# A graph-and-experts layer on one core: the first two expert lots gathered on chip instead of through DRAM, and the products for nodes without edges spread over two PSUM banks

## The chip, the cores and the metric

One core of one Trainium2 chip runs the kernel. The time is device microseconds of that core, from the start to the end of one execution; six executions of the kernel before are given. A trace of one further execution, taken by the hardware profiler, goes with them. In it PE is TensorE's matmul stream and PEld its weight loads, DVE is VectorE, ACT is ScalarE, POOL is GpSimd, SP is SyncE; a suffix q (ACTq, SPq) is the sequencer of that engine, which issues transfers.

## The reference, cut to what matters

```python
# x: 3125 x 256; src, dst: 100000 edges, sorted by dst
xn = layernorm(x)
e   = relu((xn[dst] - xn[src]) @ theta.T + theta_b + xn[src] @ phi.T + phi_b)
gnn = segment_max(e, dst)                     # one row of 256 per node, 0 where there is no edge
q, k, v = split(xn @ w_qkv.T)                 # 8 heads of 64; k and v are normalised per head
mix = (q @ (k.T @ v) / N) @ w_out.T + b_out   # attention without softmax
x = x + gnn + mix
t = layernorm(x)
p, i = top_k(softmax(t @ Wr + br), 2)         # 2 of 8 experts for each node
y_e  = gelu((t * ln_g[e] + ln_b[e]) @ W1[e] + b1[e]) @ W2[e] + b2[e]   # 256 -> 1024 -> 256
out = x + sum over the two chosen experts of (p / sum p) * y_e
```

## The kernel before

**Tiles and groups.** The 3125 nodes are 25 tiles of 128 rows (`NT`, `P`). They are cut into five groups, worked on from the last nodes to the first: `GROUPS` is ((17,25), (10,17), (4,10), (1,4), (0,1)), called group 0 to group 4 here. The edges are laid out in columns of 128, one edge per partition; group 0 takes 134 columns, the others 151, 185, 158 and 99 (`STEPS`), 727 in all.

**The edge stream.** For each column, POOL gathers 128 rows of a table `b_d` in DRAM by an indirect DMA (`gather`, L129, called at L1663), and DVE folds the row into a running maximum (`fold`, L414), six columns behind (`LAG`). Windows of 8 columns are stored to DRAM (`s_d`) by SP. Five window buffers turn. When the columns of a group are folded, `group(g)` (L1424) sends the group's tiles through `token_tile` (L483: last edge row by an indirect DMA `r1`, maximum, relu, layer norm, router logits), then `dispatch` (L1397) ranks each node among those that chose the same expert (`slots`, L589) and, for groups 0 and 1, scatters the normalised rows by POOL into a table `xs_d` in DRAM, ordered by expert (`scatter`, L136; two halves of a group, one indirect DMA per tile and choice).

**Nodes without edges.** `without_edges` (L454) computes for each tile of 128 nodes, before its tokens are handled, `xn @ theta.T + biases` and `x + mix`: one bias product, two products of 512 columns with `am_w`, and a product of x itself with an identity, which adds x inside PSUM. ACT copies both halves out (L463, L464). The PSUM tile comes from the class `Early` (L1385), which hands out the one bank that the expert stream later uses under the name `trf`.

```python
am = ps.tile([P, 2 * D], F32, name="mm")
add_bias(am, E, P, slice(0, 2 * D), True, False)
for c in range(2):
    nc.tensor.matmul(am, xnT(i, c), am_w[:, c, :], start=False, stop=False)
nc.tensor.matmul(am[:, D:2 * D], ident, x_sb[:, i, :], start=False, stop=True)
```

**The expert stream.** `Stream.go` (L895) works through lots (group, expert), 8 lots for each of groups 0 to 3. A lot has 256 places (128 in group 3). Lots are numbered u in the order they are added: 0 to 7 are group 0, 8 to 15 group 1, 16 to 23 group 2, 24 to 31 group 3. For groups 0 and 1 a pair of lots is loaded from `xs_d` in one DMA of 512 KB issued by ACT (`rows`, L807) and turned by PE transposes (`turn`, L848). For groups 2 and 3 nothing goes through DRAM (`on_chip`, L796): DVE builds a one-hot matrix per tile from the ranks (`hots`, L826), and PE multiplies the normalised rows of the group's tiles with it (`turn`, L837). Both end in the bank `trf`; ACT scales it to `xe` (`scaled`, L859). `Units.run` (L722) then does the expert: for each of 8 chunks f a first product into `hp` (L730), Gelu by ACT (L732), and, interleaved, the second products of the lot before into `yp` (L754). A program-order helper `done` stores the result to `ys_d`. `between` says what else of the next lots is issued at which f. Group 4 (one tile) goes through all 8 experts densely at the end (`dense_tile`, L973), and `combine` (L1564) gathers the stored expert rows back for the other groups.

**What sets the order.** All engines but POOL run in an order written out by hand: tasks are Python generators, each `yield n` means n ticks later, and the loop of the gathers advances the clock `now` by one tick per POOL transfer (`tick`, L1354). So a task's instructions stand on each engine's queue at a place relative to the gathers, and each engine goes through its queue in that order. The expert stream paces itself by a model of PE: `on_pe` (L92) adds an assumed cost in microseconds to `clock["pe"]` (one tick is taken as 1.25 us), and `room` (L763) keeps the stream about two ticks ahead of it. Masks for the highest-degree nodes (`first_maxima`, L1206; PE L1256, DVE L1222) are worked off between, starting when group 0 has been dispatched, and pausing while the tokens of groups 1 and 2 are handled.

**Names that matter below.** `add(g)` (L778) appends a group's 8 lots to the stream; for group 0 it is called at L1476, five ticks after the last scatter. `ring` (L161) holds 14 buffers for Gelu outputs. PSUM holds three tiles `mm`, and for the stream one `trf`, two `hp` and two `yp`.

Of the kernel before, what the change touches and what calls it, by code (L numbers as in the profile page):

```python
# [8 lines left out]
F32 = mybir.dt.float32  # L9
# [5 lines left out]
OP = mybir.AluOpType  # L15
# [4 lines left out]
P = 128  # L20
# [4 lines left out]
D = 256  # L25
# [22 lines left out]
G = len(GROUPS)  # L48
# [19 lines left out]
TICK = 1.25  # L68
ROWS = 256
SPILL = 128  # L70
APART_3 = 32
ROWS_3 = 2 * APART_3 + E + 2

# [7 lines left out]
def gps_layer(ctx: ExitStack, tc: tile.TileContext, x, src, dst, thetaT, phiT, biases, wq, wkvT,  # L81
# [372 lines left out]
    def without_edges(ps, i):  # L454

        am = ps.tile([P, 2 * D], F32, name="mm")
        add_bias(am, E, P, slice(0, 2 * D), True, False)
        for c in range(2):
            nc.tensor.matmul(am, xnT(i, c), am_w[:, c, :], start=False, stop=False)
        nc.tensor.matmul(am[:, D:2 * D], ident, x_sb[:, i, :], start=False, stop=True)  # L460
        on_pe(2.3)
        yield 3
        nc.scalar.copy(xn2(i), am[:, 0:D])  # L463
        nc.scalar.copy(x_sb[:, i, :], am[:, D:2 * D])  # L464

    def roots(work, v, y):

# [121 lines left out]
    def slots(ro, ps, g, half, i0, i1, pick, taken, chosen=None):  # L589
# [36 lines left out]
        over = ro.tile([P, nt, E], F32, name="over")  # L626
        nc.vector.tensor_scalar(over, rank, float(cap), None, op0=OP.is_ge)
        if chosen is not None:
            nc.vector.scalar_tensor_tensor(chosen[:, i0 - first:i1 - first, :], rank, 1.0, took, op0=OP.add, op1=OP.mult)
            clock["chosen", g, half] = True  # L630
            yield 1
# [26 lines left out]
        slot_f = ro.tile([P, 2, nt], F32, name="slot_f")  # L658
        nc.vector.tensor_reduce(slot_f, mine, AX.X, OP.add)
        nc.vector.tensor_scalar(from_i[:, :, i0:i1], slot_f, float(end), None, op0=OP.min)  # L660
        if chosen is not None:
            return
        out2 = ro.tile([P, nt], F32, name="out2")
        nc.vector.tensor_scalar(out2, slot_f[:, 1, :], float(end), float(of_group), op0=OP.is_ge, op1=OP.mult)
# [44 lines left out]
    class Units:  # L709
# [12 lines left out]
        def run(self, e, w1t, xe, w2t, done, between, parts, part):  # L722


            n = parts * part
            hT = []
            for f in range(FC):
                hp = self.ps.tile([P, ROWS], F32, name="hp")
                for c in range(2):
                    nc.tensor.matmul(hp[:, 0:n], w1t[:, c, f, :], xe[:, c, 0:n], start=(c == 0), stop=(c == 1))  # L730
                hT.append(self.hidden())
                nc.scalar.activation(hT[f][:, 0:n], hp[:, 0:n], AF.Gelu, bias=sm[:, 4 + f, e:e + 1])  # L732
                on_pe(n / P * 0.43)
# [33 lines left out]
    class Stream:  # L767


        def __init__(self, wts, act, ps):  # L770
            self.wts, self.act, self.ps = wts, act, ps
            self.lots, self.through, self.open = [], set(), True
            self.held = {}
            self.chosen = {}
            self.parts = []
            self.plan()

# [16 lines left out]
            return xn_hi[:, 7 + 4 * to:11 + 4 * to, :]  # L794

        def on_chip(self, u):  # L796
            return u < len(self.lots) and self.lots[u][0] >= G - 3

        def spilled(self, u):

# [4 lines left out]
                asked.append((G - 3, move(nc.scalar, to, xs_d[at:at + SPILL].rearrange("(p s) d -> p s d", s=2))))  # L805

        def rows(self, v):  # L807
            if 2 * v < len(self.lots) and ("xs", v) not in self.held and not self.on_chip(2 * v):
                xs = self.held["xs", v] = self.at(v % 2)
                asked.append((self.lots[2 * v][0], move(nc.scalar, xs.rearrange("p (k s) d -> p k s d", k=2), self.two(v))))  # L810
                for g, put in sent:
                    if g > asked[-1][0]:
                        apart_in_rows(asked[-1][1], put)

        def hots(self, u):

            if self.on_chip(u) and ("hot", u) not in self.held:
                g, e = self.lots[u]
                n, nt = CAPS[g], GROUPS[g][1] - GROUPS[g][0]
                if g == G - 3:  # L820
                    flat = xn_hi[:, 7:13, :].rearrange("p s d -> p (s d)")
                else:
                    flat = xn_lo[:, 6:9, :].rearrange("p s d -> p (s d)")[:, u % 2 * nt * n:(u % 2 + 1) * nt * n]
                hot = self.held["hot", u] = flat.rearrange("p (i n) -> p i n", n=n)
                for i in range(nt):
                    nc.vector.tensor_scalar(hot[:, i, :], place_of[g], self.chosen[g][:, i, e:e + 1], None, op0=OP.is_equal)  # L826

        def turn(self, u):
            if ("hot", u) in self.held and ("tr", u) not in self.held:
                tr = self.held["tr", u] = self.ps.tile([P, 2, ROWS], F32, name="trf", bufs=1)  # L830
                g = self.lots[u][0]
                i0, i1 = GROUPS[g]
                hot = self.held["hot", u]
                more = self.held.get(("over", u))
                for c in range(2):
                    for i in range(i0, i1):
                        nc.tensor.matmul(tr[:, c, 0:CAPS[g]], xn2(i)[:, c * P:(c + 1) * P], hot[:, i - i0, :],  # L837
                                         start=(i == i0), stop=(i == i1 - 1 and more is None), skip_group_check=True)
                    for r in range(0 if more is None else 2):
                        nc.tensor.matmul(tr[:, c, r * P:r * P + SPILL // 2], more[:, r, c * P:(c + 1) * P],  # L840
                                         ident[0:SPILL // 2, 0:SPILL // 2], start=False, stop=(r == 1), skip_group_check=True)
                on_pe(1.5 if more is None else 6.1)
            elif ("xs", u // 2) in self.held and ("tr", u) not in self.held:
                tr = self.held["tr", u] = self.ps.tile([P, 2, ROWS], F32, name="trf", bufs=1)
                n = self.half(u)
                for c in range(2):
                    for r in range(2):
                        nc.tensor.transpose(tr[:, c, r * n:(r + 1) * n],  # L848
                                            self.held["xs", u // 2][0:n, self.lots[u][1] % 2 * 2 + r, c * P:(c + 1) * P],
                                            ident[0:n, 0:n])  # L850
                on_pe(1.2)
# [43 lines left out]
        def go(self):  # L895
# [5 lines left out]
            while True:  # L901
                if u == len(self.lots):

                    for _ in units.last():
                        yield room()
                    units.behind = None
                    if u < len(self.lots):
                        continue
                    if not self.open:
                        break  # L910
                    if G - 3 in self.through:
                        nc.scalar.activation(table, eps, AF.Sqrt)
                    while u == len(self.lots):
                        yield 0.5
                    nc.scalar.activation(table, eps, AF.Gelu)
                if ("xe", u) not in self.held:
                    self.rows(u // 2)
                    self.spilled(u)
                    self.hots(u)
                    yield 8 if ("hot", u) not in self.held else 4 if ("over", u) in self.held else 1.5  # L920
                    self.turn(u)
                    yield 2
                    self.scaled(u)
                    yield 2
# [460 lines left out]
    class Early:  # L1385

        def tile(self, shape, dt, name):
            return at_hand["ffp"].tile([P, 2, ROWS], dt, name="trf", bufs=1).rearrange("p c n -> p (c n)")

    carried = {}  # L1390
    routed = set()
# [5 lines left out]
    def dispatch(g, half, i0, i1, top, top_i, taken):  # L1397
# [10 lines left out]
        if g >= G - 3:  # L1408
            yield from slots(ro, mm, g, half, i0, i1, made[0], taken, at_hand["ffn"].chosen[g])
            return  # L1410
        yield from slots(ro, mm, g, half, i0, i1, made[0], taken)
        yield BEHIND_SLOTS[g]
        put = []
        for i in range(i0, i1):
# [9 lines left out]
    def group(g):  # L1424
# [11 lines left out]
        if g >= G - 3 and g < G - 1:  # L1436
# [23 lines left out]
        for i in range(i0, i1):  # L1460
            start(routed_tile(i, last_rows(at_hand["tok"], i, rows), slices, carried, top[:, i - i0, :],
                              top_i[:, i - i0, :], newton=g == 1, at_once=2 if g > 1 else None))
            yield PER_TILE[g]
        if g == G - 2:
            while ("chosen", g, 0) not in clock:
                yield 0.5
            at_hand["ffn"].add(g)
            at_hand["ffn"].open = False
# [171 lines left out]
    def mixers():  # L1640
# [195 lines left out]
```

## Time and profile before

| what | value |
|---|---|
| median of 6 runs | 1159.2 us (1158.15 to 1163.15) |
| the profiled execution | 1161.85 us, its span 1160.0 us, granted PE clock 0.899 |
| PE busy | 897.9 us, 77% of the span |
| DVE busy | 793.9 us, 68% |
| POOL busy | 846.1 us, 73% |
| ACT busy | 331.7 us, 29% |
| the chain that ended last | PE 32%, DVE 20%, DMA 19%, POOL 16%, issue 12%, ACT 1% |

The chain's share is spread over four engines, so the span has to be read by stages: mixers and edges up to about 262 us, nodes without edges from 262 to 405 us, then the lots of group 0 (first Gelu at 436.5 us), group 1 (597.7 us), group 2 (814.7 us) and group 3 (1004.2 us), and the dense tile from 1090 us. Those stage starts are the first ACT L732 of each lot in the timeline.

### The profile page before, as it was taken

To read this page: it belongs to the slowest core of one execution; us is meant where nothing else is said; L and a number is where in the kernel's file an instruction comes from. 1 tells how busy PE (TensorE), PEld (TensorE's weight loads), DVE (VectorE), ACT (ScalarE), POOL (GpSimd) and SP (SyncE) were. 2 spreads that over 40 slices of the span, in tenths; PEclk is the share of its full clock that TensorE was granted. 3 is DMA by queue.
4 is the path that set the end of the run, shared out by engine and by line. 5 is a ranking of instruction groups with operands and counts; after the bars stand their busy time and mean duration, and the time that the engine had idled before them with its cause. 6 is when DMAs were issued, how large, how long until landed. Compare 5 with 4: busy or idle time off the path is not lost.

```text
span 1160.0 us, 14777 instructions
## 1 busy us (share of the span) xinstructions
PE 897.9 (77%) x4461; PEld 691.4 (60%) x4461; DVE 793.9 (68%) x2543; ACT 331.7 (29%) x799; POOL 846.1 (73%) x868
## 2 busy tenths in 40 slices
PE   6436888846567609989958898844999998999896
PEld 5323444423244208867747787733877786898796
DVE  7599998874567327587358787776888866733542
ACT  4310233311133103243222232331312224333342
POOL 6677777777777777777777777777777777776461
PEclk9867999978689759999889999955999999999998
DMA  8755677788776457999667899657678997898592
GB/s 271 243 171 183 213 243 272 257 296 299 269 241 209 168 197 242 337 305 314 241 240 261 309 384 322 229 176 235 216 269 305 312 334 259 295 328 327 182 346 77
DMA packets 100263, 300.96 MB, mean 259 GB/s; under 512 B 20099, under 2 KB 43002, under 8 KB 89550
## 3 DMA queue, kind: packets, MB, share of 16 engines
q0 software_dynamic: 41824, 113.70, 31.6%
q1 hardware_dynamic: 29180, 109.58, 24.4%
q10 hardware_dynamic: 29170, 76.65, 18.9%
q8 instruction: 37, 0.61, 0.2%
q14 instruction: 52, 0.43, 0.1%
HBM read 181.72 MB, written 118.13 MB: 258 GB/s over the span
## 4 chain that ended last, share of the span: by engine, by line
PE 32%; DVE 20%; DMA 19%; POOL 16%; issue 12%; ACT 1%; ACTq 0%; DVEq 0%; POOLq 0%; SPq 0%
DMA g<-b_d,srcI 18%; POOL g L129 12%; PE hp L730 9%; PE yp L754 8%; DVE g L414 6%; PE trf L837 5%; POOL xs_d L136 2%; DVE xn_hi L1222 2%; PE v L1291 2%; PE k L1291 2%; PE bp L286 1%; DMA r<-s_d,end_i 1%; PE dots_p L1314 1%; PE trf L840 1%; DVE hit L343 1%
## 5 line engine op out<-in xcount | busy, mean ns | idle before, releaser
L129 POOL DMA_INDIRECT g<-b_d,srcI x727 | 714.0, 982 | 229.4 <-issue 197.3
L414 DVE SCALAR_TENSOR_TENSOR g<-g,cut 128x256 f32<-128x256 f32 x722 | 348.5, 483 | 209.9 <-DMA g<-b_d,srcI 195.1
L732 ACT ACTIVATE ring<-hp,sm 128x256 f32<-128x256 f32 (+1 forms) x320 | 137.9, 432 | 349.2 <-PE hp L730 340.4
L730 PE MATMUL hp<-xe,big 128*128 128x256 f32 (+1 forms) x736 | 168.8, 354 | 4.7 <-issue 2.3
L754 PE MATMUL yp<-big,ring 128*128 128x256 f32 x608 | 162.9, 387 | 0.0
L1222 DVE CUSTOM_DVE_ANT_0 xn_hi<-bT,mm 128x512 bf16<-128x512 f32 (+1 forms) x224 | 140.2, 626 | 29.3 <-PE mm L1256 24.3
L730 PEld LDWEIGHTS hp<-xe,big 128*128 128x128 f32 x736 | 124.4, 194 | 20.5 <-issue 3.0
L754 PEld LDWEIGHTS yp<-big,ring 128*128 128x128 f32 x608 | 112.2, 196 | 14.6 <-issue 0.3
L730 PE MATMUL hp<-xe,w 128*128 128x256 f32 (+1 forms) x448 | 103.8, 362 | 1.3 <-ACT ring L732 0.6
L754 PE MATMUL yp<-w,ring 128*128 128x256 f32 x368 | 95.9, 380 | 0.0
L730 PEld LDWEIGHTS hp<-xe,w 128*128 128x128 f32 x448 | 77.6, 199 | 12.1 <-ACT ring L732 1.6
L754 PEld LDWEIGHTS yp<-w,ring 128*128 128x128 f32 x368 | 67.7, 191 | 9.2
L1256 PE MATMUL mm<-ident_h,absent 128*128 128x128 bf16 x400 | 38.6, 223 | 26.8 <-DVE most L1222 20.7
L129 POOL DMA_INDIRECT g<-ys_d,from_i x42 | 41.1, 979 | 24.5 <-DVE g L1577 11.1
L1256 PEld LDWEIGHTS <-absent 128*128 128x128 bf16 x400 | 28.1, 100 | 40.4 <-DVE most L1222 27.3
L837 PE MATMUL trf<-xn_hi,xn_lo 128*128 128x256 f32 x192 | 47.4, 400 | 3.7 <-DVE xn_hi L826 3.7
L859 ACT ACTIVATE xe<-trf,sm 128x256 f32<-128x256 f32 (+1 forms) x64 | 30.8, 535 | 59.9 <-PE trf L848 39.2
L507 PE MATMUL mm<-cr,oh 128*128 128x257 f32 x84 | 27.7, 449 | 22.9 <-issue 10.2
L837 PEld LDWEIGHTS trf<-xn_hi,xn_lo 128*128 128x128 f32 x192 | 37.5, 199 | 9.6 <-DVE xn_hi L826 4.0
L848 PE MATMUL trf<-ident,xn_hi 128*128 128x128 f32 x64 | 10.6, 292 | 35.1 <-DMA xn_hi<-xs_d 35.1
L1300 DVE TENSOR_REDUCE var<-big 128x16 f32<-128x1024 f32 x25 | 30.4, 1215 | 9.3 <-ACT big L1297 9.3
L1291 PE MATMUL v<-wkv,xn_hi 128*128 128x512 f32 x56 | 27.8, 618 | 10.2 <-ACT big L1296 10.2
(327 smaller groups left out, 1304.6 us busy)
## 6 DMA issues: line engine op xcount, KB each, us to landing
s_d<-g SPq DMA_DIRECT2D x75, 1024.0 KB
big<-in_w ACTq DMA_DIRECT2D x44, 512.0 KB
w<-in_w ACTq DMA_DIRECT2D x32, 512.0 KB
s_d<-g SPq DMA_DIRECT2D x13, 896.0 KB
g<-b_d,srcI POOLq DMA_INDIRECT x727, 4.0
big<-in_w ACTq DMA_DIRECT2D x4, 2048.0 KB
ys_d<-ys ACTq DMA_DIRECT2D x24, 256.0 KB
xs_d<-zero ACTq DMA_DIRECT2D x16, 256.0 KB
```

Source lines behind the costliest of these rows:

```text
L129: got = nc.gpsimd.indirect_dma_start(out=to, out_offset=None, in_=table, in_offset=row_index(index))
L414: nc.vector.scalar_tensor_tensor(g[:, j, :], last, cut[:, t:t + 1], g[:, j, :], op0=OP.add, op1=OP.max)
L507: nc.tensor.matmul(r2, picks[k], carried[g], start=(k == 0), stop=(k == len(slices) - 1))
L730: nc.tensor.matmul(hp[:, 0:n], w1t[:, c, f, :], xe[:, c, 0:n], start=(c == 0), stop=(c == 1))
L732: nc.scalar.activation(hT[f][:, 0:n], hp[:, 0:n], AF.Gelu, bias=sm[:, 4 + f, e:e + 1])
L754: nc.tensor.matmul(yp[r][0:part, :], hT[q][:, r * part:(r + 1) * part], w2t[:, q, :], start=(q == 0), stop=(q == FC - 1 and self.whole))
L837: nc.tensor.matmul(tr[:, c, 0:CAPS[g]], xn2(i)[:, c * P:(c + 1) * P], hot[:, i - i0, :], start=(i == i0), stop=(i == i1 - 1 and more is No ...
L859: nc.scalar.activation(xe[:, c, 0:n], self.held["tr", u][:, c, 0:n], AF.Identity, bias=sm[:, 2 + c, e:e + 1], scale=sm[:, c, e:e + 1])
L1222: nc.vector.tensor_tensor_reduce(unread[:, 0:n * P], bT[:, h, 0:n * P], mask_p[:, 0:n * P], 1.0, NEG, op0=OP.add, op1=OP.max, accum_out=mo ...
L1256: nc.tensor.matmul(mask_p[:, i * P:(i + 1) * P], absent[:, at:at + 1].to_broadcast([P, P]), ident_h, start=True, stop=True)
L1291: nc.tensor.matmul(to, xnT(i, c), wkv[:, c, k * INNER:(k + 1) * INNER], start=(c == 0), stop=(c == 1))
L1300: nc.vector.tensor_reduce(var, sq, AX.X, OP.add)
```

## The change

Four things are done together. The first two lots of group 0 (`AT_FIRST`) are built on chip from one-hot matrices as those of groups 2 and 3 are, with `ring` as the home of the matrices, before the scatter of group 0 has been issued; the group is added to the stream as soon as its ranks are known, and the other six lots wait for the scatter (`sent`). `without_edges` no longer multiplies x with the identity; DVE adds x when it takes the result out of PSUM, in place of an ACT copy. Its PSUM tiles are the two `hp` banks (made 512 columns wide) in place of the one `trf` bank, and a tile is issued every 3.25 ticks instead of every 3.5 (group 0) or 4.25. The cost that the model of PE takes for a turned lot of group 2 goes from 6.1 to 6.5 us. The first two lots do not start before all tiles without edges are through (`parts`).

```diff
+AT_FIRST = 2
 def without_edges(ps, i):
...
-            nc.tensor.matmul(am, xnT(i, c), am_w[:, c, :], start=False, stop=False)
-        nc.tensor.matmul(am[:, D:2 * D], ident, x_sb[:, i, :], start=False, stop=True)
-        on_pe(2.3)
+            nc.tensor.matmul(am, xnT(i, c), am_w[:, c, :], start=False, stop=(c == 1))
+        on_pe(1.9)
         yield 3
         nc.scalar.copy(xn2(i), am[:, 0:D])
-        nc.scalar.copy(x_sb[:, i, :], am[:, D:2 * D])
+        nc.vector.tensor_add(x_sb[:, i, :], x_sb[:, i, :], am[:, D:2 * D])
...
         if chosen is not None:
+            clock["chosen", g] = clock.get(("chosen", g), 0) + nt
...
-        if chosen is not None:
+        if g >= G - 3:
             return
...
-                hp = self.ps.tile([P, ROWS], F32, name="hp")
+                hp = self.ps.tile([P, 2 * ROWS], F32, name="hp")
...
-            return u < len(self.lots) and self.lots[u][0] >= G - 3
+            return u < len(self.lots) and (self.lots[u][0] >= G - 3 or u < AT_FIRST)
...
         def rows(self, v):
-            if 2 * v < len(self.lots) and ("xs", v) not in self.held and not self.on_chip(2 * v):
+            if 2 * v < len(self.lots) and ("xs", v) not in self.held and self.lots[2 * v][0] in self.sent and not self.on_chip(2 * v):
...
-                if g == G - 3:
+                if g < G - 3:
+                    flat = ring[:, 0:nt, :].rearrange("p s d -> p (s d)")
+                elif g == G - 3:
...
-                on_pe(1.5 if more is None else 6.1)
+                on_pe(1.5 if g == G - 2 else 6.5)
...
+                for k in range(AT_FIRST if u == 0 else 0):
+                    while "parts" not in clock:
+                        yield 0.5
+                    self.hots(k)
+                    yield 2.5
+                    self.turn(k)
+                    yield 5.5
+                    self.scaled(k)
+                    yield 1
                 if ("xe", u) not in self.held:
+                    while not self.on_chip(u) and self.lots[u][0] not in self.sent:
+                        yield 0.5
                     self.rows(u // 2)
...
     class Early:
         def tile(self, shape, dt, name):
-            return at_hand["ffp"].tile([P, 2, ROWS], dt, name="trf", bufs=1).rearrange("p c n -> p (c n)")
+            return at_hand["ffp"].tile([P, 2 * ROWS], dt, name="hp")
...
-        yield from slots(ro, mm, g, half, i0, i1, made[0], taken)
+        yield from slots(ro, mm, g, half, i0, i1, made[0], taken, at_hand["ffn"].chosen.get(g))
...
+        if g == 0:
+            while clock.get(("chosen", g), 0) < i1 - i0:
+                yield 0.5
+            at_hand["ffn"].add(g)
...
             yield 5 if g < G - 3 else 0.5
-            at_hand["ffn"].add(g)
+            at_hand["ffn"].sent.add(g)
+            if g:
+                at_hand["ffn"].add(g)
...
                 start(without_edges(Early(), i))
-                yield 3.5 if g == 0 else 4.25
+                yield 3.25
+        yield 3
+        clock["parts"] = True
```

More of the change, by code (lines that the diff above doesn't have):

```diff
@@ L774, in __init__ @@
             self.chosen = {}
+            self.sent = set()
             self.parts = []
@@ L825, in hots @@
                 for i in range(nt):
-                    nc.vector.tensor_scalar(hot[:, i, :], place_of[g], self.chosen[g][:, i, e:e + 1], None, op0=OP.is_equal)
+                    nc.vector.tensor_scalar(hot[:, i, :], place_of[max(g, G - 3)], self.chosen[g][:, i, e:e + 1], None, op0=OP.is_equal)
         def turn(self, u):
@@ L1435, in group @@
         slices = slices_of(g)
-        if g >= G - 3 and g < G - 1:
+        if g == 0 or G - 3 <= g < G - 1:
             at_hand["ffn"].chosen[g] = ro.tile([P, i1 - i0, E], F32, name=f"chosen{g}")
```

## The prediction

> **What bounds the kernel now.** I read the page's groups first, then the timeline of POOL, then busy time by stretches of 20 us, then PE's and DVE's timelines where PE idles.
>
> ```profile
> L129 POOL DMA_INDIRECT g<-b_d,srcI x727 | 714.0, 982 | 229.4 <-issue 197.3
> ...
> 422.57 1.55 POOL L136 DMA_INDIRECT xs_d<-xn_hi,slot_i  x1 [0.30 <-issue]
> ...
> 586.72 1.13 POOL L136 DMA_INDIRECT xs_d<-xn_hi,slot_i  x1 [0.31 <-issue]
> ...
> 1061.55 0.94 POOL L129 DMA_INDIRECT r<-s_d,end_i  x1 [3.27 <-DVE g L414]
> ```
>
> The first line is the pacemaker: 727 gathers of 982 ns, and idle before them that is nearly all "issue", so POOL waits for almost nobody. In POOL's timeline, between the first gather at 48.93 us and 1061.55 us, only two pauses are over 0.4 us (1.77 us at 165.31, 1.10 us at 552.14). I count 790 transfers from 48.93 to 1057.34, so one every (1057.34 - 48.93) / 789 = 1.278 us. POOL runs like a clock until 1061 us, and the two scatters end where that clock puts them: 422.57 (group 0) and 586.72 (group 1).
>
> ```profile
> 400.00:420.00 20.00, 2.53 (x7) 1.13 (x6) 6.06 (x13) 2.73 (x6) 15.13 (x17) 0.66 0.65 230
> 420.00:440.00 20.00, 7.80 (x34) 6.91 (x35) 3.98 (x9) 3.37 (x8) 15.43 (x16) 0.57 0.46 142
> ...
> 740.00:760.00 20.00, 13.93 (x66) 10.87 (x63) 14.85 (x56) 6.86 (x15) 15.32 (x16) 0.86 0.62 203
> 760.00:780.00 20.00, 8.59 (x30) 6.27 (x30) 15.30 (x68) 6.38 (x13) 15.24 (x16) 0.50 0.56 184
> 780.00:800.00 20.00, 4.73 (x26) 3.77 (x26) 12.52 (x56) 4.46 (x7) 15.13 (x17) 0.50 0.64 213
> ...
> 432.20 1.08 PE L848 MATMUL trf<-ident,xn_hi 128*128 128x128 f32 x4 [29.02 <-DMA xn_hi<-xs_d]
> ...
> 593.17 1.12 PE L848 MATMUL trf<-ident,xn_hi 128*128 128x128 f32 x4 [6.11 <-DMA xn_hi<-xs_d]
> ...
> 803.58 5.49 PE L837 MATMUL trf<-xn_hi,xn_lo 128*128 128x256 f32 x12 [3.69 <-DVE xn_hi L826]
> ```
>
> The stretches list PE, PEld, DVE, ACT, POOL, then granted clock, DMA share and GB/s. PE starves three times: 29.02 us before group 0 (waiting for the rows that were scattered to DRAM), 6.11 us before group 1 (the same wait), and from about 750 to 803 us before group 2, where it waits for the ranks that DVE makes from edges folded on POOL's clock. After 803 us PE is the bound: its idle time in the eight stretches from 820 to 980 us adds up to 8.9 us (4.7 of it in the last), and the dense tile at the end is PE too. So the end is (start of group 2, set by POOL's clock) plus (PE work from there).
>
> **The change, part by part.**
>
> *x added by DVE.* The identity product goes: 50 records of 410 ns, 16.3 us of PE; the 25 ACT copies L464 at 377 ns, 9.4 us; in their place 25 DVE additions. The trace has exactly one such operation, at the end:
>
> ```profile
> 1101.05 0.42 DVE L1008 TENSOR_TENSOR x_sb<-x_sb,mm 128x256 f32<-128x256 f32 x1 [2.11 <-PE mm L1007]
> ```
>
> 25 x 0.42 = 10.5 us of DVE, spread over 262 to 400 us, where DVE is busy 9 to 18 of 20 us; what follows each addition in DVE's queue is folds, and they may be late by some 25 columns before POOL runs out of window buffers (five windows of 8, six columns of lag). Nothing on the path.
>
> *Two banks, 3.25 ticks.* Tiles were issued over 8 x 3.5 + 17 x 4.25 = 100.25 ticks, now over 81.25: 19 ticks x 1.278 = 24 us earlier in the queues. The last product, at 402.58 us before, comes near 380.
>
> *Two lots on chip.* DVE: 2 x 8 one-hots at 346 ns (median of L826 at 256 columns), 5.5 us. PE: 2 x 2 x 8 products, two records each, 64 in all. L837's twelve took 5.49 us cold and 2.59 us warm, so 0.458 or 0.216 us each: 29.3 or 13.8 us, less 2 x 4 transposes of 292 ns. Ranks of group 0's second half are there at 385.5 us (DVE L627). Then one-hots 2.8, turn 6.9 to 14.6, scale 1.0, and once more (the second one-hots reuse `ring`, so they wait for the first turn), the second turn warm: 385.5 + 2.8 + 6.9 + 2.8 + 6.9 + 1.0 = 406 to 414 us for the first product of lot 0, against 434.79. Lots 0 and 1 took 8.4 and 14.7 us (first to last Gelu); they end at 429 to 437. Now a new wait: the load of lots 2 and 3 is issued by ACT behind the Gelus of lot 1, no earlier than the scatter's end (428.15 before, a tick later now). From issue to the first product it took 434.79 - 428.15 = 6.6 us, in which PE has only masks. Lot 2 starts at 436 to 444 us instead of 461; group 0 is through 17 to 25 us sooner, near 558 to 566 instead of 583 (the last second product).
>
> *What that is worth.* Group 1 waits for its own scatter, which ends at 586.72 on POOL's clock, and PE already idles 6.11 us before it. So the gap before group 1 grows from 6 to some 25 us, and nothing else moves. Were anything of group 1 to start early, the 50 us before group 2 would swallow it as well. Gain on the end: 0.
>
> *What is left past 803 us.* (1) The model of PE takes 6.5 instead of 6.1 us for group 2's eight turns: 8 x 0.4 = 3.2 us later in the queues at the end of group 2. A turn really takes 2.59 + 0.59 + 2.79 + 0.58 = 6.55 us, and lots follow each other every 24 to 26 us while masks run, against 13.8 + 6.1 us in the model plus masks, so the queue runs ahead of PE and a slower pace should only shorten it: bounds +3.2 us (PE starves by all of it) and -4.7 us (the idle of 960 to 980 us, where PE, DVE and ACT block one another over the tokens of group 3, goes). I take 0. (2) Group 0's slots yield one tick more, so scatter and masks come a tick (1.3 us) later; masks end at 981 us and are wanted at 1024, so 0. (3) POOL's clock itself: a gather takes 982 ns in the mean and 946 in the median, so it loses 727 x 36 ns = 26 us to something, while DVE is busy 793.9 us: 3.3% of DVE's busy time. DVE gets 10.5 + 5.5 = 16.0 us more: +0.5 us. Bounds: 0, and +16.0 us if each new operation held a gather for its full length. (4) The 1.10 us pause at 552 us, where DVE hung on a PE full of group 0's lots, may go: 0 to -1.1; I take 0.
>
> The Trainium skill's page "SBUF — State Buffer", section "Who interferes with whom", speaks against the change: VectorE and GpSimd share a port pair, and a VectorE operation in a two-port mode, tensor_scalar among them, shuts GpSimd out for its whole length. By that rule the one-hots would cost POOL up to 5.5 us, and the sum would be 1164 us. The additions, which read PSUM and one SBUF operand, would cost nothing by it. The row (median 946 against a minimum of 942 ns, with DVE busy two thirds of the time) shows POOL hardly blocked, and I go by the row.
>
> A second rule, the page "TensorE: Matmul & The Clock Gate", section "What's actually happening", says that PE falls to half clock after some 3.4 us idle. The longer gap before group 1 would then cost one cold start, estimated at under 2 us, which is there already (four transposes take 1.12 us at 593.17, 0.60 at 601.50). By both, the sum is the same.
>
> **Sum.** Against the profiled execution's own 1161.85 us (span 1160.0 and 1.85 around it): 0 + 0 + 0.5 + 0 gives 1162.3. That execution lies 2.65 us above the median of the runs, 1159.2, so the forecast is 1159.7 us. About 0.2%, 2.3 us, is what a measurement of this kernel tells from no change.
>
> **The rivals.** *A, forecast: the lead is swallowed by the two gaps*, 0.55. For it: POOL without pauses, and PE idle before groups 1 and 2. Its own range is 1157 to 1163, since small shifts of order past 803 us remain. That the lots do not start sooner at all, because `parts` or the ranks hold them, would give the same time and is in it.
>
> *B, slower: the new DVE work stretches POOL's clock*, 0.13. Place: 262 to 415 us. Price: a third of the 16.0 us, 5.3 us, and everything behind POOL comes that much later: 1164.5. It decides from 2.3 of the 16.0 us on. Against it: the median gather.
>
> *C, slower: the 6.5 makes PE starve in group 2*, 0.14. Price 3.2 us: 1162.4; from 2.3 us on. For it: DVE is busy 15 to 19 of 20 us there, and one-hots stand between its folds. Against it: PE 92 to 100% busy.
>
> *D, faster: the slower pace loosens the knot at 960 to 980 us*, 0.13. Of the 4.7 us idle there it saves about 3.5: 1155.7.
>
> *E, faster: the lead survives*, 0.05: if group 1 were in truth limited by group 0's lots, the 6 us PE gap would close first and about 6 us come out: 1153. Against it: the wait named at 593.17 is the DMA of group 1's own rows.
>
> **How the numbers follow.** Predicted: 1159.7 us. Of A, 0.40 stays within 2.3 us, 0.06 falls below and 0.09 above. Same: 0.40. Faster: 0.06 + 0.13 + 0.05 = 0.24. Slower: 0.09 + 0.13 + 0.14 = 0.36. The range 1154.5 to 1165 takes in A, C, D and the nearer half of B; left out are E and B's far end, some 0.1, and the unknown.
>
> **What would show it.** Right: the first Gelu of lot 0 near 406 to 416 us, lot 2's near 440, group 0 through near 562; PE idle some 20 us and more before 593, with group 1's first transposes still at about 593 and group 2's first turn at about 803.6; POOL's last edge gather at about 1057. B shows as a last gather past 1060; C as PE idle with one-hots as releaser in 820 to 960 us; D as less than 2 us of idle in 960 to 980. Wrong altogether would be a group 1 or group 2 that starts more than 3 us away from these places.

## The result, and the profile after

The changed kernel takes 1164.25 us (median; 1161.41 to 1168.42) against 1159.76 us before: ratio 1.0033, 95% interval 1.0026 to 1.0041. It is slower by 0.33%, 4.5 us. The time lies inside the forecast's range, but the likeliest case, no change, did not come. The profiled execution after has a span of 1166.2 us, 6.2 more than the one before, and so lies above its own median.

Line numbers shift by 1 to 23 (the gather is L130, first products L731, Gelu L733, combine additions L1598). The groups of the page first:

```profile
L130 POOL DMA_INDIRECT g<-b_d,srcI x727 | 714.2, 982 | 231.1 <-issue 201.6
```

Then POOL's timeline, with the last scatters of groups 0 and 1, the last edge gather, and the next transfer:

```profile
424.52 1.55 POOL L137 DMA_INDIRECT xs_d<-xn_hi,slot_i  x1 [0.30 <-issue]
...
588.03 1.05 POOL L137 DMA_INDIRECT xs_d<-xn_hi,slot_i  x1 [0.30 <-issue]
...
1058.94 0.94 POOL L130 DMA_INDIRECT g<-b_d,srcI  x1 [0.30 <-issue]
1062.05 1.00 POOL L130 DMA_INDIRECT r<-s_d,end_i  x1 [2.17 <-DVE g L415]
```

The pacemaker is unchanged: 727 gathers, 714.2 us against 714.0, mean 982 ns as before. The scatters and the last gather come 1.3 to 2.0 us later (422.57, 586.72 and 1057.34 before), of which 1.04 us stand at the first gather already (49.97 against 48.93 us), long before any changed instruction. From the first gather to the last POOL took 1008.97 us instead of 1008.41, 0.56 longer; the forecast had taken 0.5. Next the same stretches as before (PE, PEld, DVE, ACT, POOL, granted clock, DMA share, GB/s), with one more from the dense tail, and PE's timeline at the waits.

```profile
400.00:420.00 20.00, 18.89 (x88) 15.93 (x87) 8.69 (x22) 6.31 (x14) 15.24 (x16) 1.00 0.65 222
420.00:440.00 20.00, 11.12 (x65) 9.28 (x63) 5.04 (x11) 3.97 (x9) 15.62 (x15) 0.87 0.37 115
...
740.00:760.00 20.00, 14.15 (x63) 11.25 (x62) 15.13 (x57) 6.73 (x15) 15.12 (x17) 0.81 0.65 215
760.00:780.00 20.00, 7.73 (x26) 5.30 (x25) 14.76 (x63) 6.38 (x13) 15.43 (x16) 0.50 0.55 178
...
1120.00:1140.00 20.00, 12.38 (x66) 11.13 (x65) 8.29 (x20) 3.97 (x11) 9.56 (x10) 0.74 0.77 274
```

```profile
440.20 0.61 PE L1271 MATMUL mm<-ident_h,absent 128*128 128x128 bf16 x4 [9.07 <-DVE most L1237]
...
594.29 1.12 PE L852 MATMUL trf<-ident,xn_hi 128*128 128x128 f32 x4 [5.78 <-DMA xn_hi<-xs_d]
...
803.24 3.35 PE L841 MATMUL trf<-xn_hi,xn_lo 128*128 128x256 f32 x7 [3.69 <-DVE xn_hi L830]
...
1132.28 1.19 PE L731 MATMUL hp<-xe,big 128*128 128x128 f32 x4 [7.62 <-issue]
```

PE is 18.89 us busy in 400 to 420 where it was 2.53, so the two lots do start early. Groups 1 and 2 begin where they began (593.17 and 803.58 before). New is the last line, a pause of 7.62 us inside the dense tile. The start of some lots on ACT (first Gelu, us) shows where the two kernels part; 32 to 39 are the eight experts of the dense tile:

| lot | 0 | 1 | 2 | 7 | 8 | 16 | 22 | 24 | 32 | 36 | 37 | 38 | 39 |
|---|---|---|---|---|---|---|---|---|---|---|---|---|---|
| before | 436.7 | 445.5 | 461.8 | 561.6 | 598.0 | 814.9 | 948.2 | 1004.4 | 1090.8 | 1117.6 | 1124.6 | 1134.7 | 1143.7 |
| after | 411.3 | 418.2 | 461.6 | 561.9 | 599.2 | 813.8 | 957.3 | 1001.6 | 1091.2 | 1118.2 | 1133.6 | 1142.9 | 1149.9 |

(The stage starts given with the profile before, 436.5 us and so on, are some 0.2 to 0.3 us early.) Lots 0 and 1 come 25 us sooner, lot 2 does not; from there on nothing is won. In group 2 the lots fall back by 9 us (lot 22), with 14.4 us of PE idle in 820 to 980 us instead of 8.9, and catch up before the dense tile, which starts 0.3 us apart. Expert 36 is 0.6 us later, expert 37 is 9.0: the loss of this one execution arises between these two, and 6.2 us of it are left at expert 39.

**Where the lead of lots 0 and 1 goes.** VectorE's and ScalarE's timelines after:

```profile
431.52 2.05 DVE L415 SCALAR_TENSOR_TENSOR g<-g,cut 128x256 f32<-128x256 f32 x4 [13.83 <-DMA g<-b_d,srcI]
...
438.61 0.68 DVE L1237 CUSTOM_DVE_ANT_0 xn_hi<-bT,mm 128x512 bf16<-128x512 f32 x1
```

```profile
442.72 0.47 ACT L733 ACTIVATE ring<-hp,sm 128x256 f32<-128x256 f32 x1 [11.88 <-PE hp L731]
...
446.40 0.38 ACTq L122 DMA_DIRECT2D xn_hi<-xs_d  x1
```

The scatters of group 0 take POOL's queue until 426 us, so the next edge rows come late and the fold that heads VectorE's queue waits 13.83 us (12.64 before). A mask (L1237) stands behind the folds; the mask product that PE has next waits for it (the 9.07 us above); the last chunk of lot 1 stands behind that product; its Gelu runs at 442.72; and the load of lots 2 and 3 stands behind it on ACT's queue, at 446.40. In the kernel before that load was issued at 438.04, during lot 0 (428.15 was the load of lots 0 and 1); the change has also moved it behind lot 1 in the written order. Four in-order queues pass one wait on, and lot 2 starts where it always did.

**Where the 9 us at expert 37 come from.** VectorE's timeline after, from the scaling of expert 36's input (L1004) to that of expert 37's:

```profile
1116.93 0.59 DVE L1004 TENSOR_SCALAR xe<-bT,sm 128x128 f32<-128x128 f32 x2
1117.44 0.48 DVE L1598 SCALAR_TENSOR_TENSOR g<-g,share,x_sb 128x256 f32<-128x256 f32 x1
1118.80 0.48 DVE L1598 SCALAR_TENSOR_TENSOR g<-g,share 128x256 f32<-128x256 f32 x1 [0.88 <-DMA g<-ys_d,from_i]
...
1129.08 0.49 DVE L1598 SCALAR_TENSOR_TENSOR g<-g,share,x_sb 128x256 f32<-128x256 f32 x1 [1.68 <-DMA g<-ys_d,from_i]
1131.04 0.48 DVE L1598 SCALAR_TENSOR_TENSOR g<-g,share 128x256 f32<-128x256 f32 x1 [1.47 <-DMA g<-ys_d,from_i]
1131.44 0.48 DVE L1031 SCALAR_TENSOR_TENSOR xn_hi<-yp,full,xn_hi 128x256 f32<-128x256 f32 x1
1131.84 0.60 DVE L1004 TENSOR_SCALAR xe<-bT,sm 128x128 f32<-128x128 f32 x2
```

Between the two scalings stand eight additions of `combine`, seven of which wait for a gathered row, 0.9 to 1.7 us each. Nothing in the scaling of expert 37 needs them; it is only behind them. PE resumes at 1132.28, 0.44 us after the scaling begins; the profile's "issue" beside its pause names no releaser, but this order and the times fit. In VectorE's written order, 30 of the tail's 48 additions stand ahead of the scaling for expert 36 and 38 ahead of that for expert 37; before, it was 24 and 32. So there were eight between the two scalings before, too, but six fewer had to be done in all, and the scaling for expert 37 came while PE still had products of expert 36, up to 1124.05 us:

```profile
1123.19 0.60 DVE L989 TENSOR_SCALAR xe<-bT,sm 128x128 f32<-128x128 f32 x2
```

### The profile page after: what moved, and what is told of

It is laid out like the page before. It is cut to its first block, busy times and chain, and to the rows that moved or that the text cites. A ratio compares the mean times of both kernels' runs of the same rounds, so it can differ in the third digit from the quotient of the medians.

```text
span 1166.2 us, 14808 instructions
## 1 busy us (share of the span) xinstructions
PE 911.4 (78%) x4467; PEld 696.3 (60%) x4467; DVE 808.9 (69%) x2586; ACT 328.6 (28%) x777; POOL 844.7 (72%) x868
## 4 chain that ended last, share of the span: by engine, by line
PE 30%; DMA 20%; DVE 18%; POOL 18%; issue 12%; ACT 2%; ACTq 0%; DVEq 0%; POOLq 0%; SPq 0%
DMA g<-b_d,srcI 19%; POOL g L130 15%; PE hp L731 9%; PE yp L755 8%; DVE g L415 5%; PE trf L841 3%; PE v L1306 2%; POOL xs_d L137 2%; PE k L1306 2%; DVE xn_hi L1237 1%; PE bp L287 1%; PE dots_p L1329 1%; DVE tiles L1214 1%; DVE hit L344 1%; ACT big L1311 1%
## 5 line engine op out<-in xcount | busy, mean ns | idle before, releaser
L130 POOL DMA_INDIRECT g<-b_d,srcI x727 | 714.2, 982 | 231.1 <-issue 201.6
L733 ACT ACTIVATE ring<-hp,sm 128x256 f32<-128x256 f32 (+1 forms) x320 | 137.9, 432 | 358.8 <-PE hp L731 357.9
L731 PE MATMUL hp<-xe,big 128*128 128x256 f32 (+1 forms) x736 | 172.7, 360 | 8.0 <-issue 7.6
L1237 DVE CUSTOM_DVE_ANT_0 xn_hi<-bT,mm 128x512 bf16<-128x512 f32 (+1 forms) x224 | 140.2, 626 | 21.9 <-PE mm L1271 17.4
L731 PEld LDWEIGHTS hp<-xe,big 128*128 128x128 f32 x736 | 128.6, 200 | 24.4 <-issue 9.4
L731 PE MATMUL hp<-xe,w 128*128 128x256 f32 (+1 forms) x448 | 98.9, 349 | 0.6 <-ACT xe L863 0.6
L755 PE MATMUL yp<-w,ring 128*128 128x256 f32 x368 | 98.8, 389 | 0.0
L731 PEld LDWEIGHTS hp<-xe,w 128*128 128x128 f32 x448 | 75.2, 192 | 9.6 <-ACT xe L863 0.9
L130 POOL DMA_INDIRECT g<-ys_d,from_i x42 | 40.8, 970 | 27.8 <-issue 11.3
L1315 DVE TENSOR_REDUCE var<-big 128x16 f32<-128x1024 f32 x25 | 30.4, 1215 | 9.3 <-ACT big L1312 9.3
L137 POOL DMA_INDIRECT xs_d<-xn_hi,slot_i x28 | 28.9, 1032 | 8.5 <-issue 8.2
```

Source lines behind the costliest of these rows:

```text
L130: got = nc.gpsimd.indirect_dma_start(out=to, out_offset=None, in_=table, in_offset=row_index(index))
L137: put.append(nc.gpsimd.indirect_dma_start(out=table, out_offset=row_index(index), in_=of, in_offset=None))
L755: nc.tensor.matmul(yp[r][0:part, :], hT[q][:, r * part:(r + 1) * part], w2t[:, q, :], start=(q == 0), stop=(q == FC - 1 and self.whole))
L1237: nc.vector.tensor_tensor_reduce(unread[:, 0:n * P], bT[:, h, 0:n * P], mask_p[:, 0:n * P], 1.0, NEG, op0=OP.add, op1=OP.max, accum_out=mo ...
L1315: nc.vector.tensor_reduce(var, sq, AX.X, OP.add)
```

## The experiments

Nothing is left out of the computation in any of them. Each is compared with the kernel before on the same chip.

**Undoing or adding single edits.** The theories here: T, the loss sits in the dense tail, by VectorE's order; C, the rival C of the prediction; L, the lots on chip cost it. First, the kernel after with the old 6.1:

```diff
-                on_pe(1.5 if g == G - 2 else 6.5)
+                on_pe(1.5 if g == G - 2 else 6.1)
```

> The changed kernel with one number put back: the model of PE takes 6.1 us again for a turned lot of group 2. Theory T (the 4.5 us are lost in the dense tile at the end, where on VectorE's queue the scaling of the dense tile's next input stands behind two more of the additions that bring the stored expert rows back): in this kernel the order of the tail on VectorE's queue is that of the kernel before (8 additions, then the first scalings), so about 1160 us, ratio 0.999 to 1.001, and the seventh dense expert's first Gelu within 8 us of the sixth's, where it was 15.4 us (1117.9 to 1133.3) in the changed kernel. Theory C (the slower pace starves PE in group 2): also about 1160 us. Theory L (the two lots on chip cost it): stays at 1164 us.

Measured: 1162.43 us, ratio 1.0025 (1.0005 to 1.0045). The 0.4 us make at most part of the loss. What T expected of the tail came: the gap between experts 36 and 37 is 7.1 us, with VectorE's order of before. Its time, 0.999 to 1.001, did not, and lot 22 still comes late, at 954.7 us.

Second, the kernel before with 6.5:

```diff
-                on_pe(1.5 if more is None else 6.1)
+                on_pe(1.5 if more is None else 6.5)
```

> The kernel before with one number changed: 6.5 us instead of 6.1 in the model of PE. Theory C: slower, about 1164 us (8 x 0.4 = 3.2 us and more). Theory T: the order of the tail on VectorE's queue is that of the kernel before, so about 1160 us, ratio 0.999 to 1.001. Theory L: 1160 us.

Measured: 1158.31 us, 0.9986 (0.9966 to 1.0007). The 0.4 us of charge, which this edit adds for seven lots (lot 17 is left out, as explained below), cost nothing: theory C falls for them, as the prediction had priced it.

Third, the kernel after without lots of group 0 on chip:

```diff
-AT_FIRST = 2
+AT_FIRST = 0
```

> The changed kernel with AT_FIRST = 0: no lot of group 0 on chip, all else as changed. Theory L: back to about 1160 us. Theory T: the order of the tail on VectorE's queue is that of the changed kernel, so it stays at about 1164 us (ratio 1.003), and the long stall before the seventh dense expert stays. Theory C: stays at 1164 us.

Measured: 1169.3 us, 1.0075 (1.0048 to 1.0101). Theory L falls: without the lots on chip the kernel is slower still. T had expected 1164 us. The gap between experts 36 and 37 is 11.9 us, with VectorE's order of after; but the dense tile, too, starts 5.0 us late, at 1095.8 us.

Fourth, the kernel before with the new parts alone (addition by VectorE, two banks, 3.25 ticks):

```diff
-        nc.tensor.matmul(am[:, D:2 * D], ident, x_sb[:, i, :], start=False, stop=True)
...
-        nc.scalar.copy(x_sb[:, i, :], am[:, D:2 * D])
+        nc.vector.tensor_add(x_sb[:, i, :], x_sb[:, i, :], am[:, D:2 * D])
...
-            return at_hand["ffp"].tile([P, 2, ROWS], dt, name="trf", bufs=1).rearrange("p c n -> p (c n)")
+            return at_hand["ffp"].tile([P, 2 * ROWS], dt, name="hp")
...
-                yield 3.5 if g == 0 else 4.25
+                yield 3.25
```

> The kernel before with the nodes without edges done as changed (two hp banks in turn, x added by VectorE, a tile every 3.25 ticks), no lot on chip, 6.1 us in the model. Theory T: the order of the tail is that of the changed kernel, so about 1164 us (ratio 1.003). Theories C and L: 1160 us.

Measured: 1167.86 us, 1.0078 (1.0047 to 1.0108). T had expected half of this loss, and by the order of the tail after, which is not there: 32 additions stand ahead of expert 37, as before. In its trace the first turn of group 2 comes at 806.25 us instead of 803.58; the rest of the loss does not show, since that execution, 1165.19 us, is the fastest of this kernel.

**The charge by itself.** The charge is what `on_pe` adds to the model's clock for a turn. Read again, its edit holds more than 0.4 us. Lot 17, the second of group 2, has no spill, so `more is None` charged it 1.5; `g == G - 2` is group 3, so the change charges lot 17 the full 6.5. That is 5.0 + 7 x 0.4 = 7.8 us of model time, and what the stream writes later moves back by some ticks against the gathers. (The kernel with 6.1 above still charged lot 17 as the change does, 6.1 for 1.5. And the condition reaches lots 0 and 1 on chip, which also have no spill: 6.5 each in the kernel after, 1.5 each in the next run and in the lots alone.) This became theory M; P says that the parts make the loss.

```diff
 # the kernel after
-                on_pe(1.5 if g == G - 2 else 6.5)
+                on_pe(1.5 if more is None else 6.1)
```

> The kernel after, with the model's charge for a turn as it was before (1.5 where a lot has no spill, else 6.1). Theory M (the model): lot 17, the second of group 2, has no spill, so the kernel before charged its turn 1.5 us and the change charges it 6.5; with the other seven that is 7.8 us of model time, and everything written behind the third lot of group 2 comes five folds later, in another order. It expects the order of before in group 2 and in the dense tail, lot 22 at about 948 us instead of 957, PE's idle in 820 to 980 us near 9 us instead of 14.4, and a median of 1159 to 1161.5 us. Theory P (the loss is made by the parts before 400 us and the charge is a bystander, as the kernel with 6.1 at 1162.4 suggests): 1163 us or more.

Measured: 1161.44 us beside 1160.71 before, 1.0004 (0.9986 to 1.0021). The loss is gone. Lot 2 starts at 460.7 us (461.6 after), so the lower charge for lots 0 and 1 moved little there. Lot 22 starts at 946.2 us, PE's idle in 820 to 980 us is 7.35, experts 36 and 37 are 7.1 us apart. Its VectorE timeline from the scaling for expert 37 to that for expert 38:

```profile
1119.41 0.60 DVE L1004 TENSOR_SCALAR xe<-bT,sm 128x128 f32<-128x128 f32 x2
1120.76 0.48 DVE L1598 SCALAR_TENSOR_TENSOR g<-g,share,x_sb 128x256 f32<-128x256 f32 x1 [0.76 <-DMA g<-ys_d,from_i]
1123.07 0.48 DVE L1598 SCALAR_TENSOR_TENSOR g<-g,share 128x256 f32<-128x256 f32 x1 [1.83 <-DMA g<-ys_d,from_i]
...
1129.14 0.59 DVE L1004 TENSOR_SCALAR xe<-bT,sm 128x128 f32<-128x128 f32 x2
```

The same waits for gathers are there, but the scaling for expert 37 now stands ahead of them, and PE has that expert to work on meanwhile. It pauses only 2.45 us, before expert 38.

```diff
 # the kernel before
-                on_pe(1.5 if more is None else 6.1)
+                on_pe(1.5 if g == G - 2 else 6.5)
```

> The kernel before, with nothing changed but the charge for a turn (1.5 in group 3, 6.5 in all of group 2, so also for lot 17). Theory M: the order of after in group 2 and in the dense tail, so the loss of after: 1162.5 to 1165 us, PE's idle in 820 to 980 us near 14 us. Theory P: 1159.7 us, as before.

Measured: 1164.18 us, 1.0031 (1.0017 to 1.0045): this one line, alone, makes the loss of the whole change (1.0033). It has no lot on chip and the old parts. It differs from the kernel with 6.5 above (0.9986) by the charge of lot 17 alone. Its PE timeline has the pause of the kernel after, again ended 0.44 us after the scaling of expert 37 begins (1128.51):

```profile
1128.95 1.20 PE L730 MATMUL hp<-xe,big 128*128 128x128 f32 x4 [7.23 <-issue]
```

PE's idle in 820 to 980 us is 10.56 us, not the 14 expected, and the dense tile starts at 1088.5 us, earlier than before's 1090.8. So in this execution the delay of group 2 is made good, and the loss is in the tail.

**The lots by themselves.** The kernel after with the parts and the charge of before:

```diff
-        nc.vector.tensor_add(x_sb[:, i, :], x_sb[:, i, :], am[:, D:2 * D])
+        nc.scalar.copy(x_sb[:, i, :], am[:, D:2 * D])
...
-                yield 3.25
+                yield 3.5 if g == 0 else 4.25
...
-                on_pe(1.5 if g == G - 2 else 6.5)
+                on_pe(1.5 if more is None else 6.1)
```

> The kernel after, with the parts as before (identity product, ACT copy, one bank, 3.5 and 4.25 ticks) and the charge as before: only the first two lots on chip are new. The forecast's own step (the lead is swallowed by the gaps before groups 1 and 2): 1159.7 us and group 2's first turn at 803.6. If the lots win some 5 us (the kernel after against the one with no lot on chip): 1155 us, and POOL's pause at 552 us shorter. With the parts late (last product near 402 us) the lots' lead should be smaller than in after: first Gelu of lot 0 at 412 to 425 us.

Measured: 1161.57 us, 1.0005 (0.9988 to 1.0023). The first Gelu came at 433.6 us, later than any of the expected places. The rest is the more telling: lot 2 starts at 473.4 us, 11.6 late, lot 7 at 570.0, lot 8 at 608.1, lot 15 at 736.4, 10.5 late. And then group 2:

```profile
801.78 5.49 PE L842 MATMUL trf<-xn_hi,xn_lo 128*128 128x256 f32 x12 [3.94 <-DVE xn_hi L831]
```

It starts at 801.78 us, 1.8 earlier than before. Ten microseconds late in groups 0 and 1 are swallowed whole by the gap before group 2.

**The parts again.** The fourth kernel with its pace set back to 3.5 and 4.25 ticks:

```diff
-                yield 3.25
+                yield 3.5 if g == 0 else 4.25
```

> The kernel before with the parts changed but for their pace: x added by VectorE, two banks, no identity product, still a tile every 3.5 and 4.25 ticks. If the pace of 3.25 makes the loss of the parts (1167.9 in the kernel with all of it): 1159 to 1161 us. If the additions or the banks make it: 1164 us or more. A loss through POOL's clock would show as a last edge gather past 1058.8 us, one through group 2's start as a first turn past 805 us.

Measured: 1164.58 us, 1.003 (1.0008 to 1.0053). Neither clean case: it overlaps the loss with the new pace. Its last edge gather and first turn of group 2 (803.50 us) are where they were, so neither place named holds the loss. In its trace the tail stalls one expert later, by another chain: a gather of `combine` waits long for its buffer,

```profile
1127.89 0.95 POOL L129 DMA_INDIRECT g<-ys_d,from_i  x1 [9.86 <-DVE g L1576]
```

and experts 37 and 38 start 15.0 us apart, with VectorE's written order that of before.

**The tail with the scaling on ScalarE, and the pace alone.** To separate the order on VectorE's queue (theory Q, the T of above) from the idle among group 2's lots (theory G), the scaling was moved to an engine that has no additions; and, for the parts, the kernel before got the pace alone (`yield 3.25`).

```diff
-                    nc.vector.tensor_scalar(held["xe", e][:, c, 0:P], xT[:, c, :], sm[:, c, e:e + 1],
-                                            sm[:, 2 + c, e:e + 1], op0=OP.mult, op1=OP.add)
+                    nc.scalar.activation(held["xe", e][:, c, 0:P], xT[:, c, :], AF.Identity, bias=sm[:, 2 + c, e:e + 1],
+                                         scale=sm[:, c, e:e + 1])
```

> The kernel after, with the scaling of the dense tile's input (16 operations, two for an expert) done by ScalarE instead of VectorE. Theory Q (the charge costs by the order on VectorE in the dense tail: the scaling for expert 37 stands behind combine additions that wait for gathers): the gap of 15 us between the first Gelus of experts 36 and 37 falls to some 7, nothing else moves, and the median is 1157 to 1161 us. Theory G (the charge costs by PE's idle among the lots of group 2, 14.4 instead of 8.9 us): the tail's gap moves or vanishes, but the time stays at 1162.5 us or more.

> The kernel after with the charge as before, and the scaling of the dense tile's input on ScalarE. Theory Q: with the scaling off VectorE's queue the charge no longer matters, so this takes the same time as the kernel after with the scaling on ScalarE, within 1.5 us. Theory G: this one is faster by about 4 us. If both are right in part, some 2 us. Against the kernel before: 1155 to 1160 us, since stalls of the dense tail by chance go too.

> The kernel before, with nothing changed but the pace of the parts: a tile every 3.25 ticks for all groups instead of 3.5 and 4.25; identity product, ACT copy and the one bank stay. If the pace makes a loss that the parts show without lots on chip (1167.9 with all of it, 1164.6 with the old pace): 1162 to 1165 us and group 2's first turn past 805 us. If additions or banks make it: 1159 to 1161.5 us.

> The kernel after with the scaling of the dense tile's input on ScalarE, once more, beside a kernel before that takes its usual 1160 us (beside the first run of it the kernel before took 1627 us). Theory Q (the charge costs by the order on VectorE in the dense tail): no gap over 9 us between the first Gelus of experts 36 to 39, and a ratio to the kernel before of 1.000 or less. Theory G (it costs by PE's idle among the lots of group 2): the gap is gone but the ratio stays at 1.002 to 1.004, as with the charge of 6.1 (1.0025), in which the tail had the order of before.

All four runs were made on two chips on which the kernel before itself took 1627 and 1633 us, 40% more. There: after with the scaling on ScalarE 1.0168 (1.011 to 1.0226) on the one and 1.0049 (1.0013 to 1.0084) on the other; with the charge set back too, 1.0058 (1.0011 to 1.0104); the pace alone 0.9938 (0.9887 to 0.9989). The first kernel's two intervals do not even meet, and the expectations were made for another balance of waits.

One thing that both Q and G expected did not come: with the scaling on ScalarE the gap between experts 36 and 37 was 16.0 and 15.3 us, not some 7. But it was another gap. In the first of the two traces the scaling for expert 37 begins at 1600.46 us and PE starts that expert only at 1613.91, since it pauses inside expert 36, the longest time for 3.42 us before 1610.34. The pace alone, with the order of before and the scaling on VectorE, has such a gap of 14.9 us, too, with a pause of 6.01 us inside expert 36. What PE waits for there the profiles do not name. These runs settle nothing, on Q and G or on the pace. On a chip with before at its usual time none of the three was tried.

**What the traces say on Q and G.** From the first Gelu of expert 36 to that of expert 39, in all kernels profiled beside a before of 1160 us, by the order that VectorE's queue has in the tail (one execution each):

| order in the tail | kernel: us |
|---|---|
| as before (32 additions ahead of expert 37; lots alone 30) | before 26.1; before with 6.5 25.7; after with 6.1 26.6; charge back 26.3; lots alone 25.0; parts 26.3; parts, old pace 31.2 |
| as after (38 ahead) | after 31.8; after without lots on chip 28.6; before with the charge 30.4 |

Charge against no charge on the kernel before is 30.4 - 26.1 = 4.3 us there, and its runs lost 1164.18 - 1160.71 = 3.5 us. That the edit of the charge makes the loss is shown by adding it and by taking it back. That the tail holds the loss is seen in the traces and fits in size, but it is not shown by an experiment of its own: one that takes the additions out of the way on an ordinary chip is missing, and the last kernel of the first row stalls as long in the order of before. And 6.1 in the kernel after, with the tail in the order of before and group 2's lots late, still measured 1.0025, down to 1.0005: so some of the loss, by that kernel's median 2.6 us (1162.43 against 1159.8), may sit among those lots.

## Why the prediction was right or wrong

**What bounds the kernel: right up to the dense tile.** Group 1 started at 594.29 us (forecast about 593) and group 2 at 803.24 (about 803.6). That the stretches before them swallow what happens to group 0 is shown from the other side by the lots alone: 10 us late there, nothing in the time. POOL's transfers in the stretch that was counted are 781 in the trace, not 790, so one takes 1.293 us and not 1.278; the terms built on it hardly move. What the forecast had wrong is that the dense tile "is PE too": after, PE stood still in it for 7.62 us behind VectorE's queue.

**The lots' early start: right; its continuation: wrong, without consequence.** Lot 0 came at 411.3 us (406 to 416), though the tiles without edges were through at 389.1 us and not near 380. The step "Lot 2 starts at 436 to 444 us" failed, since lots 0 and 1 did not end at 429 to 437: lot 1 hung from 431 to 440 us on a mask product, and the load behind it was issued at 446.40 (the forecast's sum has it by 437). The forecast counted masks as PE's only other work there, and did not ask what the masks wait for. So group 0 was through no sooner (lot 7 at 561.9), and the gap before group 1 stayed at 5.78 us instead of growing past 20.

**The model's charge: the step that failed.** The forecast wrote "The model of PE takes 6.5 instead of 6.1 us for group 2's eight turns: 8 x 0.4 = 3.2 us later in the queues at the end of group 2", and took 0. Two things were wrong in it. The edit was read by its number and not by its condition, which lot 17 meets differently: 7.8 us of model time, not 3.2. And its price was looked for at PE in group 2, while a later place in the queues changes who stands behind whom everywhere after, here in the dense tail. Measured by itself, it is 1.0031; seven of the eight times 0.4 alone are 0.9986. In the sum, the term 0 should have been about +3.5 us. That the time still fell inside the range, near its upper end, is luck: that end was there for B and C, and neither made the loss.

**Rivals.** A's gaps could have swallowed the lead, as the lots alone show with a delay, but in the kernel after they had none to swallow: it ended at lot 2 already. And the term beside it moved the time. B fell: 25 additions (10.4 us, mean 416 ns) and 16 one-hots more on VectorE left 727 gathers at 714.2 us, 714.0 before. The Trainium skill's page "SBUF — State Buffer", section "Who interferes with whom", says that VectorE and GpSimd lock each other out of a shared port pair while an operation such as tensor_scalar runs in a two-port mode. Whether these one-hots ran in such a mode no run shows; the gathers' totals show no lock of 5.5 us. (The forecast's sum by that rule comes to 1164.7 us, not 1164.) C had the right line and sign; PE did idle 5.5 us more in 820 to 980 us, but the dense tile started only 0.3 us later. D did not come: 960 to 980 us still has 20 - 17.42 = 2.58 us of idle, and the time went up. E fell at lot 2.

**The parts: priced at nothing, open.** With the two lots on chip they cost nothing that is seen (charge back: 1.0004); without them they cost 1.003 to 1.0078. Where the parts lose is open; one trace has a loss at group 2's start, another in the tail. Nor do the pieces add: without lots on chip the parts alone (1.0078) and the parts with the charge (1.0075) measured the same within their intervals of some 0.003 to each side, though the charge alone costs 1.0031.

## What to carry to other kernels

Where a written order is steered by a model of time, an edit of the model is an edit of every queue behind it: work out for which items its condition changes, not only its number, and compare the written orders to the end of the program. As the tail's traces suggest, an operation that the bound engine needs next should not stand in a queue behind operations that wait for transfers; how many stand ahead of it can be counted. A lead ends at the first in-order queue whose head waits for something else, so follow each moved step to its next load before writing its gain.

## What the runs showed of the hardware

A short pause can cost PE its clock, and a longer one need not. PE's timeline of the kernel before, at the first products behind three pauses; the last two rows are later products behind the third:

```profile
633.20 0.40 PE L1256 MATMUL mm<-ident_h,absent 128*128 128x128 bf16 x4 [2.91 <-DVE most L1222]
...
1090.04 2.13 PE L730 MATMUL hp<-xe,big 128*128 128x128 f32 x14 [2.29 <-DVE xe L989]
...
1133.37 1.19 PE L730 MATMUL hp<-xe,big 128*128 128x128 f32 x4 [2.30 <-issue]
...
1135.21 1.06 PE L730 MATMUL hp<-xe,big 128*128 128x128 f32 x4
...
1137.73 0.61 PE L730 MATMUL hp<-xe,big 128*128 128x128 f32 x4
```

Four products that take 0.61 us took 1.19 and 1.06 after 2.30 us of idle, and the granted clock is 1.00 in 1130.00 to 1133.30 us and 0.50 in 1133.40 to 1136.70. After the 7.62 us of the kernel after they took 1.19, 1.06, 1.06 and 0.89. But after 2.91 us of idle four mask products took 0.40 us, where four of the same form took 0.61 behind the 9.07 us pause at 440.20 us after; and in 629.00 to 635.00 us, as in 1087.00 to 1093.00 around the pause of 2.29 us, the granted clock is 1.00. The Trainium skill, "TensorE: Matmul & The Clock Gate", section "What's actually happening", puts the fall at some 3.4 us without work; here one pause of 2.30 us was enough and one of 2.91 was not.

And two chips in this study ran the kernel before 40% slower. A changed kernel's page from one of them (after with the scaling on ScalarE):

```profile
L130 POOL DMA_INDIRECT g<-b_d,srcI x727 | 705.2, 970 | 549.1 <-issue 240.0
```

The gather itself takes 970 ns, against 982 elsewhere, but POOL is idle 549.1 us before them instead of 231.1, and the mean granted clock of PE is 0.784 instead of 0.890. Why, no run shows. A ratio measured there weighs other waits than one measured at 1160 us.
